# Query-normed attention: the Newton steps of its two unit lengths issued in GpSimd's list instead of VectorE's

## The chip, the cores and the metric

The kernel runs on one core of a Trainium2 chip. The metric is the device time of one execution, in microseconds (us); the median of several executions is quoted. The core has four compute engines that work side by side, each through its own list of instructions in order: TensorE (PE, matrix products and transposes), VectorE (DVE), ScalarE (ACT, activations and copies) and GpSimd (POOL). PEld in the profile is TensorE's weight load, SP the engine that issues most DMAs. An instruction that waits holds up everything behind it in its engine's list.

## What is computed

A decoder of four blocks of three sublayers on a stream X of 32 sequences of 128 tokens, 128 features each, all float32. Each sublayer adds its output to X. The change lies in the third sublayer ("L0f"), an attention whose softmax is normed over the queries, followed by two products, each scaled to rows of unit length, and a GELU:

```python
x = x + L0_ffn(layernorm(x), Wq, Wk, Wv, Wo, Wff)
def _l2_normalize(z):
    n = jnp.linalg.norm(z, axis=-1, keepdims=True)
    return z / jnp.maximum(n, EPS)
def L0_ffn(x, Wq, Wk, Wv, Wo, Wff):          # 16 heads of 8
    q, k, v = split_heads(x @ Wq), split_heads(x @ Wk), split_heads(x @ Wv)
    scores = jnp.einsum('bqd,bkd->bkq', q, k) / jnp.sqrt(D)
    attn = jax.nn.softmax(scores, axis=-1)    # over the queries
    out = jnp.einsum('bkq,bkv->bqv', attn, v)
    z = merge_heads(out) @ Wo
    z = _l2_normalize(z)
    z = z @ Wff
    z = _l2_normalize(z)
    return jax.nn.gelu(z, approximate=False)
```

## The kernel before

The first five sublayers run as one software pipeline, the method `stream`. Its unit of work is one sequence n; four sequences make a group g, so L0f has 32 sequences in 8 groups. The pipeline counts steps t. In step t the scores of sequence t are made, and each of the other functions works on an earlier or a later sequence, by the offsets in the two tuples `after` and `ahead`. A function of a group runs when the last (for `after`) or first (for `ahead`) sequence of the group is at its offset, so each runs every fourth step.

The order on every engine is the order in which the program is written. While `stream` runs, each engine is wrapped in a `Lane` (its call is line 1350, which is why nearly all instructions of the profile carry that line) that ties every instruction to the one written before it for that engine.

```python
after = ((last, 11), (units, 10), (third, 9), (second, 8), (units, 6), (closed, 5), (features, 4))
ahead = ((turned, 5), (queries, 3), (keyed, 2), (valued, 1), (normed, 9))
```

For a sequence of L0f (kind "keys"):

- `scores` makes its scores (PE, tile `sc`), takes the exponential (ACT, tile `PT`, two instructions) and adds the two halves of the queries on GpSimd (tile `half`, two instructions of 128x512).
- `summed`, one step later, finishes that sum on VectorE (tile `rcs`: a reduction and a reciprocal) and has GpSimd multiply the values by it (tile `vs`).
- `values`, another step later, multiplies `PT` by `vs` on PE (tile `av`).

For a group: `closed` (Wo) and `third` (Wff) make a product, which ACT copies to `z` and squares with sums of rows to `ss`. `units`, one step later, calls `unit` (lines 1699 to 1706): VectorE clamps `ss`, calls `rsqrt` (line 1814) for the reciprocal root of four numbers on each partition, and multiplies each of the four 128x128 pieces of `z` by its column of the result. `units` stands in `after` twice, at 10 and at 6: in one step the second unit length of an older group is made and then the first unit length of a younger one. Such a step is called a slot here. The eight groups make nine slots, four steps apart: the first and the last with one call, the seven between with two. Behind the calls of a slot, VectorE's list has half of `queries` (tile `qTm`), then `summed` of the sequence before; GpSimd's list has `half` of the slot's own sequence, then `vs` of the sequence before. In front of the slot GpSimd's list has `half` of the sequence before and `vs` of the one before that.

`rsqrt` takes a first guess by integer arithmetic in `guess` (line 1806, two VectorE instructions, tile `ry`) and refines it by three Newton steps on the engine that it is given, with a scratch tile `rt`. VectorE, which is the default, takes three instructions a step, GpSimd four. The same helper is already given GpSimd elsewhere in the kernel (line 2129 for four numbers a partition, lines 2023 and 2324 for 32).

Of the kernel before, what the change touches and what calls it, by code (L numbers as in the profile page):

```python
# [1366 lines left out]
class Fast(General):  # L1367
# [125 lines left out]
    def stream(self, stages, context=False, fresh=False):  # L1493

        tc, plain = self.tc, self.nc
        nc = self.nc = Ordered(plain, tc)
        M = NB * len(stages)
        with ExitStack() as es:
            wk = es.enter_context(tc.tile_pool(name="st", bufs=2))
# [199 lines left out]
            def unit(s, name):  # L1699

                nc.vector.tensor_scalar(s["ss"], s["ss"], 1e-24, None, ALU.max)
                rn = self.rsqrt(wk, s["ss"], "u")
                z = wk.tile([128, 4, 128], F32, tag=name, name=name)
                for j in range(4):
                    nc.vector.tensor_scalar(z[:, j, :], s["z"][:, j, :], rn[:, j:j + 1], None, ALU.mult)
                return z
# [23 lines left out]
            def units(g):  # L1730
                st, s = T[g // 8], G[g]
                if st["kind"] == "keys":
                    s["unit"] = unit(s, "z1")
# [39 lines left out]
            for t in range(-9, M + 12):  # L1773
# [22 lines left out]
                if fresh:  # L1796
                    for k in range(2):
                        u = t - (M - NB + 8 * k + 13)
# [1438 lines left out]
```

## Time and profile before

| what | value |
|---|---|
| median of 3 executions | 5677.57 us (5674.41 to 5685.71) |
| the profiled execution | 5680.26 us |
| its span in the profile | 5678.4 us |
| PE busy | 5087.1 us (90%) |
| DVE busy | 4253.1 us (75%) |
| POOL busy | 3060.6 us (54%) |
| ACT busy | 2941.2 us (52%) |
| L0f's slots in the trace | from 335 to 533 us |

A timeline row has the start in us, the length in us, the engine, the line, the operation, the tiles (out<-in), the shapes and the number of instructions merged into the row; in brackets, how long the engine sat idle before it and what ended that. A waits row has the waiting engine and tile, what ended the wait, the total in us, how often, and the longest. A windows row has a stretch, its length, and the busy time of PE, PEld, DVE, ACT and POOL in it with the number of instructions, then TensorE's granted clock (1.00 is full), the DMA share and GB/s.

### The profile page before, as it was taken

The page shows a single profiled execution, that of the slowest core. Times are in us where ns is not written, and L with a number is a line of the kernel's source. Part 1 is how long each engine was busy: PE and PEld are TensorE (multiplying, and loading weights), DVE is VectorE, ACT ScalarE, POOL GpSimd, SP SyncE. Part 2 cuts the span into 40 slices and gives each one's busy share as a digit, 9 for nine tenths or more (in the row PEclk, how much of TensorE's full clock was granted, in tenths as well). Part 3 has the DMA queues.
Part 4 walks back from the last instruction along what each step waited for, and adds up shares of the span by engine and source line. Part 5 has one row for each costly group of instructions (what it writes and reads, how often), then busy time and mean ns, then how long its engine had stood idle before and what let it go on. Part 6 is the DMA issues. An engine that isn't in the chain of part 4 may idle for free.

```text
span 5678.4 us, 143610 instructions
## 1 busy us (share of the span) xinstructions
PE 5087.1 (90%) x56814; PEld 3545.0 (62%) x56814; DVE 4253.1 (75%) x11590; ACT 2941.2 (52%) x4126; POOL 3060.6 (54%) x4772
## 2 busy tenths in 40 slices
PE   8978976877868998986899999999999999999998
PEld 4544556755646666663666666666666666666665
DVE  5587642255538999986888888888888888888885
ACT  5767642334425555543455555555555555555553
POOL 0041011021015555546777777777777777777774
PEclk9989977888989999998999999999999999999999
DMA  1000065324002222212334444444444444444442
GB/s 50 2 1 2 24 202 164 99 64 116 5 20 52 52 55 50 50 40 56 63 62 85 83 76 72 80 78 73 70 83 76 70 80 80 71 70 72 73 74 52
DMA packets 1807430, 376.01 MB, mean 66 GB/s; under 512 B 1681458, under 2 KB 1786393, under 8 KB 1805726
## 3 DMA queue, kind: packets, MB, share of 16 engines
q1 hardware_dynamic: 1797376, 330.90, 28.8%
q10 hardware_dynamic: 4766, 19.06, 1.0%
q0 software_dynamic: 4608, 16.78, 0.9%
q8 instruction: 451, 7.39, 0.6%
q14 instruction: 229, 1.88, 0.1%
HBM read 124.02 MB, written 41.16 MB: 29 GB/s over the span
## 4 chain that ended last, share of the span: by engine, by line
PE 36%; DVE 12%; SPq 8%; POOL 5%; DMA 4%; issue 4%; ACT 2%; DVEq 0%; ACTq 0%; POOLq 0%
SPq L2039 7%; PE sc L1350 6%; PE y L1350 6%; PE av L1350 5%; PE qk L1350 5%; PE vp L1350 4%; DMA qkT<-bt 3%; POOL rt L1350 2%; DVE bt L1350 2%; POOL raw L1350 2%; PE gp L1350 2%; PE oTp L1350 2%; PE ap L1350 1%; DVE ss L1350 1%; DVE neg L1350 1%
## 5 line engine op out<-in xcount | busy, mean ns | idle before, releaser
L1350 POOL TENSOR_TENSOR raw<-raw,rt 128x1024 f32<-128x1024 f32 x384 | 899.7, 2364 | 0.0
L1350 POOL TENSOR_TENSOR raw<-raw,ry 128x2048 f32<-128x2048 f32 x224 | 811.7, 3624 | 14.0
L1350 PE MATMUL qk<-wqkv,zs 128*128 128x512 f32 x1536 | 725.0, 594 | 7.0 <-DVE raw L1350 7.0
L1350 ACT ACTIVATE sq<-qk 128x1024 f32<-128x1024 f32 x448 | 458.8, 1024 | 363.4 <-PE qk L1350 152.6
L1350 POOL TENSOR_TENSOR rt<-ry 128x32 f32<-128x32 f32 (+1 forms) x864 | 200.3, 232 | 794.1 <-DVE ry L1350 685.2
L1350 DVE TENSOR_REDUCE ss<-sq 128x16 f32<-128x1024 f32 x448 | 532.6, 1194 | 52.0 <-ACT sq L1350 52.0
L1350 DVE TENSOR_TENSOR rt<-qk,tab 128x1024 f32<-128x1024 f32 x384 | 468.4, 1220 | 59.4 <-ACT sq L1350 38.7
L1350 DVE STREAM_TRANSPOSE bt<-raw 128x1024 f32<-128x1024 f32 x384 | 455.3, 1221 | 71.4 <-POOL raw L1350 44.7
L1350 DVE TENSOR_TENSOR raw<-qk,tab 128x1024 f32<-128x1024 f32 x384 | 466.3, 1214 | 0.0
L1350 ACT ACTIVATE PT<-sc 128x1024 f32<-128x1024 f32 x384 | 373.3, 1029 | 127.9 <-PE sc L1350 126.0
L1350 PEld LDWEIGHTS qk<-wqkv,zs 128*128 128x128 f32 x1536 | 274.2, 191 | 263.4 <-issue 255.2
L1350 ACT ACTIVATE P<-sc 128x1024 f32<-128x1024 f32 x384 | 373.3, 1022 | 119.6 <-PE sc L1350 119.1
L1350 ACT COPY oT<-oTp 128x512 f32<-128x512 f32 x384 | 208.7, 589 | 437.4 <-PE oTp L1350 437.4
L1350 PE MATMUL sc<-qkT 64*128 64x128 f32 x6144 | 406.7, 283 | 7.1 <-DMA qkT<-bt 1.4
L1350 PEld LDWEIGHTS sc<-qkT 64*128 64x128 f32 x6144 | 374.5, 193 | 58.8 <-issue 53.4
L1350 PE MATMUL vp<-wqkv,zs 128*128 128x512 f32 x768 | 403.7, 607 | 1.4 <-DVE raw L1350 1.4
L1350 PE MATMUL av<-va,P 128*64 128x65 f32 x12288 | 401.6, 223 | 0.0
L1350 PE MATMUL y<-wo,oT 128*128 128x128 f32 x3072 | 389.9, 280 | 0.0
L1350 PEld LDWEIGHTS av<-va,P 128*64 128x64 f32 x12288 | 375.0, 137 | 23.2 <-issue 0.2
L1350 PEld LDWEIGHTS y<-wo,oT 128*128 128x128 f32 x3072 | 362.2, 192 | 41.8 <-issue 23.9
L1350 ACT COPY va<-vp 128x1024 f32<-128x1024 f32 (+1 forms) x232 | 218.1, 940 | 211.6 <-PE vp L1350 211.3
L1350 POOL TENSOR_TENSOR X<-X,brep 128x512 f32<-128x512 f32 x24 | 30.5, 1272 | 503.9 <-DVE xn L1350 503.9
(414 smaller groups left out, 10754.6 us busy)
## 6 DMA issues: line engine op xcount, KB each, us to landing
qkT<-bt SPq DMA_DIRECT2D x3072, 64.0 KB
rows<-scr SPq DMA_DIRECT2D x32, 672.0 KB
tup<-whole SPq DMA_DIRECT2D x32, 512.0 KB
gt<-tup SPq DMA_DIRECT2D x64, 256.0 KB
tab<-in_tdo SPq DMA_DIRECT2D x32, 512.0 KB
T<-flt SPq DMA_DIRECT2D x16, 1024.0 KB
wqkv<-in_dqkv ACTq DMA_DIRECT2D x6, 1536.0 KB
scr<-dots SPq DMA_DIRECT2D x128, 66.0 KB
```

Source lines behind the costliest of these rows:

```text
L1350: self.last = call(*a, **k)
L2039: nc.sync.dma_start(out=qkT[r:r + 32, :, j, :], in_=bt[32 * j:32 * j + 32, o])
```

## The change

`unit` hands `rsqrt` GpSimd as the engine of the Newton steps. The clamp of `ss`, the two instructions of the guess and the four scalings of `z` stay on VectorE.

```diff
             def unit(s, name):
 
                 nc.vector.tensor_scalar(s["ss"], s["ss"], 1e-24, None, ALU.max)
-                rn = self.rsqrt(wk, s["ss"], "u")
+                rn = self.rsqrt(wk, s["ss"], "u", nc.gpsimd)
                 z = wk.tile([128, 4, 128], F32, tag=name, name=name)
                 for j in range(4):
                     nc.vector.tensor_scalar(z[:, j, :], s["z"][:, j, :], rn[:, j:j + 1], None, ALU.mult)
```

The helper, unchanged:

```python
def rsqrt(self, wk, v, name, eng=None, y=None):
    nc, n = self.nc, v.shape[-1]
    eng = eng or nc.vector
    y = self.guess(wk, v, name) if y is None else y
    t = wk.tile([128, n], F32, tag="rt" + name, name="rt")
    for _ in range(3):
        eng.tensor_tensor(t, y, y, ALU.mult)
        if eng is nc.gpsimd:
            eng.tensor_tensor(t, t, v, ALU.mult)
            eng.tensor_scalar(t, t, -0.5, 1.5, ALU.mult, ALU.add)
            eng.tensor_tensor(y, t, y, ALU.mult)
        else:
            eng.scalar_tensor_tensor(t, t, -0.5, v, ALU.mult, ALU.mult)
            eng.scalar_tensor_tensor(y, t, 1.5, y, ALU.add, ALU.mult)
    return y
```

## The prediction

> **What bounds the stage now.** The change touches only L0f, so I looked for its nine slots first (VectorE's rows on the tile `ss`: 335.3, 353.5, 380.2, 405.9, 432.4, 459.1, 486.0, 506.4 and 529.3 us) and then read the busy times by stretch, from one slot's second scaling to the next one's, and the waits from 330 to 540 us.
>
> ```profile
> 416.50:443.00 26.50, 20.66 (x196) 12.35 (x196) 22.44 (x70) 16.52 (x34) 11.75 (x12) 0.75 0.00 1
> 443.00:469.80 26.80, 17.45 (x200) 10.38 (x196) 24.29 (x70) 20.35 (x37) 11.89 (x12) 0.93 0.01 2
> ...
> PEld av L1350 <- POOL vs L1350: 58.1, 18, 7.9
> POOL half L1350 <- ACT PT L1350: 41.7, 13, 4.9
> PE av L1350 <- POOL vs L1350: 41.5, 17, 7.1
> POOL vs L1350 <- DVE rcs L1350: 40.1, 13, 7.0
> ```
>
> A group takes some 26.5 us, and VectorE (the third busy time) fills 22 to 24 of them; PE, ACT and GpSimd have room. PE waits for `vs`, GpSimd makes `vs` when VectorE has made `rcs`, and VectorE comes to that `rcs` only behind the slot. So the loop runs through the slot in VectorE's list. The chain that ended last begins only at 1673 us and says nothing here; but from 540 to 700 us PE is busy 151.8 of 160 us, so what is lost in L0f isn't made up behind it.
>
> GpSimd is half idle, which looks like room for the Newton steps. What decides is where they stand in its list. VectorE's rows of the slot at 432 us, then GpSimd's:
>
> ```profile
> 432.52 0.17 DVE L1350 TENSOR_SCALAR ry<-ss 128x4 int32<-128x4 int32 x1
> 432.72 0.17 DVE L1350 TENSOR_SCALAR ry<-ry 128x4 int32<-128x4 int32 x1
> 432.92 0.16 DVE L1350 TENSOR_TENSOR rt<-ry 128x4 f32<-128x4 f32 x1
> ...
> 434.70 3.10 DVE L1350 TENSOR_SCALAR z<-z,ry 128x128 f32<-128x128 f32 x4
> ...
> 437.90 1.23 DVE L1350 TENSOR_SCALAR ry<-ss 128x4 int32<-128x4 int32 x1
> ...
> 442.17 0.87 DVE L1350 TENSOR_SCALAR z<-z,ry 128x128 f32<-128x128 f32 x4
> 442.96 1.41 DVE L1350 TENSOR_SCALAR qTm<-qp,c_small 128x512 f32<-128x512 f32 x2
> ```
>
> ```profile
> 434.86 2.49 POOL L1350 TENSOR_TENSOR half<-PT 128x512 f32<-128x512 f32 x2 [3.58 <-ACT PT L1350]
> 437.30 0.41 POOL L1350 TENSOR_TENSOR vs<-v,rcs 128x128 f32<-128x128 f32 x1
> 437.84 2.50 POOL L1350 TENSOR_TENSOR half<-PT 128x512 f32<-128x512 f32 x2
> ```
>
> The first guess is ready at 432.89. In front of the slot in GpSimd's list stand a `half` and a `vs`; this `half` waits for ACT until 434.86 and the `vs` ends at 437.71. Newton steps written into that list start there, 4.8 us after VectorE is ready for them. The next `half` (437.84) is written behind the slot and will start behind its Newton steps.
>
> The rows also show a collision. Four scalings take 0.87 us alone and 3.10 while `half` runs; a guess takes 0.17 alone and 1.2. VectorE gets about one such instruction through for each `half` instruction of 1.25 us. The reduction (1.2 us) and `qTm` (1.4 us) keep their lengths beside `half`.
>
> **What is removed and added.** Sixteen calls, each 9 VectorE instructions at a pitch of 0.197 us (from 432.92, the first, to 434.70, the scalings behind: 1.78 us): 28 us off VectorE's busy time. Each gets 12 GpSimd instructions. Their form exists later in this trace, four numbers a partition behind the same guess:
>
> ```profile
> 2588.41 0.17 DVE L1350 TENSOR_SCALAR ry<-ry 128x4 int32<-128x4 int32 x1
> 2588.66 0.20 POOL L1350 TENSOR_TENSOR rt<-ry 128x4 f32<-128x4 f32 x1 [8.70 <-DVE ry L1350]
> ...
> 2591.76 0.20 POOL L1350 TENSOR_TENSOR ry<-rt,ry 128x4 f32<-128x4 f32 x1
> ```
>
> So 0.08 us from guess to first instruction and 3.30 from there to the root (2588.66 to 2591.96). The way back to VectorE I put at 0.05: `half` ended at 430.92 and the reduction waiting for it started at 430.95. A root costs 3.43 us where it cost 1.78. It is the same work on the path, slower, and nothing covers it: behind the guess VectorE's list has the scalings, which need the root, and behind them the second call, `qTm` and `rcs`, for which `vs` and PE wait.
>
> **A slot with two calls.** From the end P of the `vs` in front: 0.08 + 3.30 + 0.05 to the first root, 0.87 for its scalings (GpSimd is idle then, as its next instruction waits for the second guess), 0.59 for the clamp and the second guess, 0.08 + 3.30 + 0.05 to the second root: 8.32 us. Then GpSimd starts the held-back `half` in the same moment as VectorE the second scalings, and these take 3.10 as in the row at 434.70: P + 11.42. At 432 us that is 437.71 + 11.42 = 449.13, where the second scalings ended at 443.04: +6.1.
>
> The Trainium skill speaks against this placing as well ("SBUF — State Buffer", section "Who interferes with whom"): of a VectorE instruction in a 2-port mode and a GpSimd instruction, whoever issues first has the shared ports for the whole instruction and the other blocks fully. The row at 434.70 agrees with it (3.10 against 0.87 us); by the rule, an order in which all scalings issue first would save the difference, and the sum would be that of the first rival below.
>
> The other slots by the same sum, with P and the end of the second scalings as they are: 353 us: 358.69 + 11.42 against 364.24, +5.9; 380 us: 384.18 against 390.64, +5.0; 406 us: 411.26 against 416.53, +6.1; 459 us: 463.09 against 469.81, +4.7. (In those of 380 and 459 us VectorE's Newton instructions themselves collided with `half` before, 1.2 us instead of 0.16, which the change takes away; that is in their smaller loss.) The first slot has one call, its guess ready at 337.54 and P at 337.52: 337.54 + 3.43 + 3.10 = 344.07 against 340.22, +3.9. The six: 31.7 us.
>
> Does each loss pass on whole? From the `vs` behind a slot (445.92) to the next P (463.09) are 17.2 us of PE, ACT and GpSimd: `av`, transposes and products, scores, squares on ACT, exponentials, `half`, all in order behind that `vs`. VectorE needs from 445.5 (its `rcs`) to 459.6 for its own way to the next guess and will go on to wait 3.5 us or more there. So P moves with `vs`, and every slot adds its own loss.
>
> **The last three slots** have no `half` behind them, as the next sublayer has none. At 486 us VectorE ends at 486.71 + 9.19 = 495.90 (scalings at 0.87 here) instead of 492.57. PE's transposes wait for the bank that `qTm` frees (494.1, now 497.3), but the product behind them already waited 2.45 us for ACT's copy until 497.64, and now starts at about 498.6: +1. At 506 us VectorE is 3.3 late, `qTm` done at 517.5, and PE wants that bank at 517.70: 0. At 529 us one call, +1.6, of which PE's wait for ACT at 539.4 leaves some 0.5 to 1. Bounds for the three: 0 and 8.3 (3.3 + 3.3 + 1.6); I take 2, by the waits just read.
>
> **The clock.** PE's wait for `vs` grows by the slot's loss. The granted clock is already down in these stretches (0.75 and 0.93 above): behind the 6.8 us wait at 394 us `av` took 1.93 us where 1.08 is its usual length. Behind the 3.1 us wait at 367.8 it took 1.59, so one slot may still get slower. I take 0.5; the bounds are 0 and 1.3 a slot (the spread of `av`, products and scores behind the waits at 367.8 and 420.1), 5 at most.
>
> The Trainium skill ("TensorE: Matmul & The Clock Gate", section "Part 1: The HAM clock gate") has the array fall to half rate after an idle window of about 3.4 us; an estimate by it is the same, since all slots but the first two are past that already.
>
> **The sum.** 31.7 + 2 + 0.5 = 34 us. On the profiled execution that is a span of 5678.4 + 34 = 5712 and a time of 5680.3 + 34 = 5714. That execution stands 2.7 us above the median of the three, so the forecast for the median is 5677.6 + 34 = 5711.6, or 0.6% slower; 5711 in round numbers.
>
> **Rivals.** First: the second scalings don't collide, because VectorE gets its four through before `half` starts, or ACT brings that `half` late. Each of the first six slots is then 2.2 us better: 34 - 13.4 = 21, time 5698. Against it stand three of the double slots before (355.8, 408.3 and 434.7), where scalings that began up to 0.2 us ahead of `half` still took 3.1. In the same direction lies some slack that I don't see between slots.
>
> Second, heavier: the cold PE and the last three slots cost their upper ends, 31.7 + 8.3 + 5 = 45, time 5723.
>
> Third, hidden: VectorE's list isn't what sets the pace and the delays go into existing waits; the 10% that VectorE is idle speaks for it. Then only a few us remain: 5678 to 5686. Against it: PE's 41.5 us of waits for `vs`, the longest right behind the slots.
>
> Fourth, on the other side: P comes ahead of the guess. The place is the `half` in front of the slot. If VectorE's later arrival let ACT and GpSimd run ahead until that `half` and `vs` end before the guess, a double slot would take 9.19 us from the guess, 432.89 + 9.19 = 442.08 against 443.04: a gain of about 1 in each of five, as the collisions go. The point from which it decides is P 4 to 5 us earlier relative to the guess. With 2 lost at the end it gives 5677.6 - 5 + 2 = 5675. Against it: that `half` waits for an exponential which is downstream of the last slot's `vs`. That the Newton steps don't move isn't possible: the wrapped engine that `unit` passes is the one `rsqrt` compares with, so its four-instruction branch is taken.
>
> **Chances.** Forecast 0.60, first rival 0.20, heavier 0.09, hidden 0.07, fourth 0.04. About 0.2%, 11 us, is what a measurement of this kernel can tell from no change. Forecast, first and heavier are all slower by more, 0.88 with a little taken off for the first's lower end; hidden and most of the fourth are within, 0.09; faster by more than 11 us has no mechanism here, 0.03. The range takes in the first rival and most of the unknown ends: 5692 to 5721.
>
> **What would show it.** Right: GpSimd's `rt<-rt,ss` of 128x4 in 48 rows from 337 to some 565 us, the first of each double slot directly behind a `vs`; VectorE idle before `z` for about 8 us (first call) and 3.4 (second), released by GpSimd's `ry`; second scalings of 3.1 us beside `half`; groups of 30 to 33 us instead of 26.5; PE's waits for `vs` up by 25 us or more; rows from 700 us on alike, shifted. Wrong: second scalings of 0.87 (first rival); Newton rows that start right at the guess (fourth); groups still at 26.5 us (hidden).

## The result, and the profile after

| | before | changed |
|---|---|---|
| median | 5677.57 us (5663.06 to 5687.01, 7 runs) | 5704.45 us (5697.33 to 5714.75, 7 runs) |
| span of the profiled execution | 5678.4 us | 5702.7 us |
| DVE busy | 4253.1 us | 4219.8 us |
| POOL busy | 3060.6 us | 3091.2 us |

The change makes the kernel slower: the ratio of the times is 1.005, with a 95% interval of 1.0035 to 1.0065, which is 20 to 37 us. VectorE did get 33 us of work less, and that bought nothing.

Busy times by stretch, changed kernel, each from the end of one slot's second scalings to the next one's (the columns as in the table before: PE, PEld, DVE, ACT, POOL, clock):

```profile
402.40:433.40 31.00, 18.80 (x196) 11.04 (x196) 18.00 (x52) 18.30 (x35) 16.50 (x36) 0.78 0.01 2
433.40:465.60 32.20, 21.31 (x196) 12.35 (x196) 17.27 (x52) 18.30 (x35) 16.36 (x36) 0.71 0.00 1
```

A group takes 31 to 32 us instead of 26.5, and no engine is busy for more than two thirds of it. VectorE, which filled 22 to 24 of 26.5 us, has 17 to 19 of 31 to 32. Who waits, from 330 to 570 us:

```profile
PEld av L1350 <- POOL vs L1350: 81.1, 18, 12.0
DVE z L1350 <- POOL ry L1350: 76.9, 16, 8.4
PE av L1350 <- POOL vs L1350: 65.2, 17, 11.2
```

The second row is new: VectorE stands 76.9 us in front of its 16 sets of four scalings, waiting for GpSimd's root. PE's wait for `vs` went from 41.5 to 65.2 us, by 24 us, most of the loss.

One slot (the one at 432 us before), VectorE's timeline and then GpSimd's:

```profile
449.61 0.17 DVE L1350 TENSOR_SCALAR ry<-ry 128x4 int32<-128x4 int32 x1
457.99 0.88 DVE L1350 TENSOR_SCALAR z<-z,ry 128x128 f32<-128x128 f32 x4 [8.21 <-POOL ry L1350]
...
459.19 0.17 DVE L1350 TENSOR_SCALAR ry<-ry 128x4 int32<-128x4 int32 x1
462.74 2.88 DVE L1350 TENSOR_SCALAR z<-z,ry 128x128 f32<-128x128 f32 x4 [3.38 <-POOL ry L1350]
```

```profile
451.88 2.49 POOL L1350 TENSOR_TENSOR half<-PT 128x512 f32<-128x512 f32 x2 [3.71 <-ACT PT L1350]
454.32 0.41 POOL L1350 TENSOR_TENSOR vs<-v,rcs 128x128 f32<-128x128 f32 x1
454.69 0.20 POOL L1350 TENSOR_TENSOR rt<-ry 128x4 f32<-128x4 f32 x1
...
462.51 0.20 POOL L1350 TENSOR_TENSOR ry<-rt,ry 128x4 f32<-128x4 f32 x1
462.66 2.48 POOL L1350 TENSOR_TENSOR half<-PT 128x512 f32<-128x512 f32 x2
```

The guess is ready at 449.78. GpSimd takes it up at 454.69, behind a `half` that waited for ACT's exponential and behind a `vs`. VectorE waits 8.21 us for the first root and 3.38 for the second. GpSimd's next `half` then starts at 462.66 beside the second scalings, which take 2.88 us where the first took 0.88.

Where the loss arises, by the end of the second scalings of each slot (the only scalings in the first and the last) in the two traces: +1.6 us at the first slot, then 5.4, 4.8, 5.2, 5.7 and 5.0 in the five double slots with half-sums, 3.2, 0.5 and 0.4 in the last three: 31.7. The first gather of the sublayer behind (GpSimd's first indirect DMA into the tile `whole`) starts at 694.6 us before and at 725.0 after: +30.4. The tile's rows, before and changed (durations in ns, then the first and the last start in us):

```profile
L1350 POOL DMA_INDIRECT whole<-in_tup,rows x32: 935/939/1150, 694.6 to 932.2; - x32
L1350 POOL DMA_INDIRECT whole<-in_tup,rows x32: 932/936/1147, 725.0 to 962.8; - x32
```

From there to the end the two traces take 4983.8 and 4977.7 us; the same stretch varies from 4968 to 4984 us in the experiments, in no order, so the difference of 6 us lies within the scatter behind the changed stage. The gather is therefore the sharper gauge, and it is used below.

### The profile page after: what moved, and what is told of

It is laid out like the page before. It is cut to its first block, busy times and chain, and to the rows that moved or that the text cites. A ratio compares the mean times of both kernels' runs of the same rounds, so it can differ in the third digit from the quotient of the medians.

```text
span 5702.7 us, 143664 instructions
## 1 busy us (share of the span) xinstructions
PE 5082.3 (89%) x56814; PEld 3543.1 (62%) x56814; DVE 4219.8 (74%) x11446; ACT 2942.4 (52%) x4126; POOL 3091.2 (54%) x4964
## 5 line engine op out<-in xcount | busy, mean ns | idle before, releaser
L1350 POOL TENSOR_TENSOR rt<-ry 128x4 f32<-128x4 f32 (+1 forms) x912 | 208.3, 228 | 841.6 <-DVE ry L1350 729.9
L1350 PEld LDWEIGHTS y<-wo,oT 128*128 128x128 f32 x3072 | 362.1, 192 | 42.0 <-issue 24.3
```

What stands on the lines that cost most here:

```text
L1350: self.last = call(*a, **k)
```

## The experiments

All are edits of the changed kernel or of the kernel before, and all compute the same. Their diffs are shortened ("..." marks lines left out). First in one table. "Stage" is the time from GpSimd's first `half` to the first gather, against that of before (694.6 - 297.0 = 397.6 us). "A group" is the mean of the five intervals between the clamps of the second to the seventh slot. The ratio comes from runs side by side with the kernel before (its median was 5673.36 us beside e1 to e4, 5677.91 beside e5 and b1 to b3, 5677.28 beside b4 and b5) and isn't exactly the quotient of the medians.

| kernel | first `half` | first gather | stage | a group | median, ratio to before (95%) |
|---|---|---|---|---|---|
| before | 297.0 | 694.6 | 0 | 26.5 | |
| changed | 297.1 | 725.0 | +30.3 | 31.7 | 1.0050 (1.0035 to 1.0065) |
| e1 front half-sum behind | 297.2 | 718.7 | +23.9 | 29.4 | 5691.68, 1.0041 (1.0027 to 1.0054) |
| e2 second call only | 297.1 | 704.1 | +9.4 | 27.8 | 5682.43, 1.0017 (1.0008 to 1.0026) |
| e3 first call only | 299.0 | 718.9 | +22.3 | 30.0 | 5690.71, 1.0035 (1.0022 to 1.0049) |
| e4 own half-sum last | 297.1 | 718.4 | +23.7 | 29.5 | 5692.9, 1.0037 (1.0023 to 1.0051) |
| e5 both held back | 297.2 | 710.6 | +15.8 | 27.7 | 5688.76, 1.0021 (1.0012 to 1.003) |
| b1 before, own half-sum last | 297.0 | 693.8 | -0.8 | 24.9 | 5674.5, 0.9999 (0.999 to 1.0008) |
| b2 before, joint root | 297.3 | 685.0 | -9.9 | 24.3 | 5665.8, 0.9981 (0.9972 to 0.9989) |
| b3 before, joint, own last | 297.1 | 680.4 | -14.3 | 23.1 | 5664.09, 0.9978 (0.9968 to 0.9987) |
| b4 before, joint, late | 297.4 | 705.2 | +10.2 | 25.4 | 5684.44, 1.0008 (0.9999 to 1.0017) |
| b5 joint, late, GpSimd | 300.4 | 715.9 | +17.9 | 27.1 | 5697.61, 1.0032 (1.002 to 1.0043) |

The times of a kernel scatter by some 10 us, so the traces carry the fine differences, one trace for each kernel. The stage and the ratio, taken of 5677.57 us, agree within 4 us in all rows but b4's (+10.2 and +4.5).

**The two calls apart.** e2 leaves the older group's call (the first of a slot) on VectorE, e3 the younger group's:

```diff
-                    s["unit"] = unit(s, "z1")
+                    first = "unit" not in s
+                    s["unit"] = unit(s, "z1", nc.gpsimd if first else None)      # e3: if not first
```

> Newton steps on GpSimd only in the call for the younger group (the second of a double slot, the only one of the first slot); the older group's stay on VectorE. Theory: GpSimd is past its waiting half-sum by the time of the second guess, so a double slot loses only the slower root less the collision it avoids, 1.6 to 1.7 us, the first slot 1.6, the last ones 1.6 in all: gather at 694.6 + 11.5 = 706 us, time 11 us above before. Rival (each call costs the same): half of the whole loss, 15 us: 710 us.

> Newton steps on GpSimd only in the call for the older group (the first of a double slot, the only one of the last slot). Theory: this call carries the wait for the half-sum, and the next half-sum then collides with the first scalings: 2.8 to 4.3 us in each of the five double slots (18 in all), nothing in the first slot, 2 in the last ones: gather at 694.6 + 20 = 715 us, time 20 us above before. Rival (each call costs the same): 15 us, 710 us.

Stages of +9.4 and +22.3 us, against the 11.5 and 20 of the theory and 15 each of the rival; their sum, 31.7, is close to the whole change. Eight calls with the same 12 instructions each cost more than twice as much in the one place as in the other. So the instructions alone don't decide: 12.9 us of the loss is the difference between the two places.

**The half-sum in front taken away (e1).** The `half` of the sequence before the slot is written behind the slot's calls (`halved` has the two additions that stood in `scores`, and `E[n]` is the sequence's `PT`):

```diff
-                    for h in (slice(0, 8), slice(8, 16)):
-                        nc.gpsimd.tensor_tensor(half[:, h], PT[:, h, 0:64], PT[:, h, 64:128], ALU.add)
+                    if n % 4 == 0: held.append(n)
+                    else: halved(n, PT)
...
+                if t % 4 == 1:                          # behind the functions of `after`
+                    while held:
+                        n = held.pop()
+                        halved(n, E[n])
```

> The changed kernel, with one thing moved: the half-sum of the sequence before a slot is written into GpSimd's list behind the slot's Newton steps instead of in front of them. Theory (the place in the list: Newton steps wait 0 to 5 us for that half-sum and its wait for ACT): the first root of a double slot follows its guess by 3.4 us, the slot ends guess + 8.3 + 2.9 us (the second scalings still collide, now with this half-sum), a loss against the kernel before of 1.0 to 1.2 us in each of the five double slots with half-sums, 1.6 to 2 in the first, some 3 in the last three: the first gather of the stage behind (694.6 us before, 725.0 with the change) at about 704 us, and the time about 10 us above the kernel before. Rival (the slow GpSimd instructions, 12 at 0.28 us for 9 at 0.20 on the path, 1.65 us in each of 16 calls): no part of the loss depends on the place, the gather stays at 720 to 725 us.

The stage lost 23.9 us: neither the 10 of the theory nor the 25 and more of the rival. The wait did go: VectorE waits 3.39 us for each first root instead of about 8. But GpSimd's and VectorE's rows behind the second root of a slot show what came in its place:

```profile
427.80 0.20 POOL L1350 TENSOR_TENSOR ry<-rt,ry 128x4 f32<-128x4 f32 x1
427.95 4.92 POOL L1350 TENSOR_TENSOR half<-PT 128x512 f32<-128x512 f32 x4
428.04 4.92 DVE L1350 TENSOR_SCALAR z<-z,ry 128x128 f32<-128x128 f32 x4 [3.38 <-POOL ry L1350]
```

Two half-sums are now held back by the Newton steps, run back to back, and the four second scalings sit among them for 4.92 us. My expectation had counted one of the two. Of a group's 5.2 us, e1 takes back 2.3.

**The other collision taken away (e4).** The slot's own `half` is written behind the `vs` of `summed`, so that it can't start before VectorE is through:

```diff
+                    if n % 4 == 1: held.append(n)
+                    else: halved(n, PT)
...
                     summed(t - 1)
+                while held:
+                    n = held.pop()
+                    halved(n, E[n])
```

> The changed kernel, with the half-sum of the slot's own sequence written into GpSimd's list behind the multiplication by the sums of the sequence before, so that it no longer starts beside the second scalings. Theory: the second scalings take 0.87 us instead of 2.87 and each of the five double slots gets 2.0 us shorter, passed on whole: gather at 725 - 10 = 715 us, time about 17 to 20 us above the kernel before. Rival (the collision isn't on the path that sets the pace, or the later half-sum makes a new wait as long): 722 to 727 us.

The gather came at 718.4, a gain of 6.6 us; the theory had 10, the rival 0. A slot's two scalings now read alike:

```profile
455.38 0.88 DVE L1350 TENSOR_SCALAR z<-z,ry 128x128 f32<-128x128 f32 x4 [6.64 <-POOL ry L1350]
...
460.13 0.87 DVE L1350 TENSOR_SCALAR z<-z,ry 128x128 f32<-128x128 f32 x4 [3.38 <-POOL ry L1350]
```

The group shrinks by 2.2 us, as expected (31.7 to 29.5). What is missing of it at the gather was lost ahead of these five groups: the first slot's clamp starts 2 us later than in the changed kernel (337.36 against 335.39), and the second slot's comes 22.9 us behind it instead of 19.7. The half-sums of the steps in front were moved too; VectorE's reductions at 305.5 and 326.7 us wait 2.38 and 3.08 us for them.

**Both held back (e5).** The edit of e1 with one condition more, and e4's place for the slot's own half-sum:

```diff
-                    if n % 4 == 0: held.append(n)
+                    if n % 4 < 2: held.append(n)
...
                     summed(t - 1)
+                while t % 4 == 1 and held:
+                    n = held.pop()
+                    halved(n, E[n])
```

> The changed kernel with both orders of the earlier runs: the half-sum in front of a slot goes behind its Newton steps, and the slot's own half-sum behind the multiplication by the sums. Theory: what the first experiment still lost was the two half-sums running back to back beside the second scalings (4.92 us there); with one of them gone these take 2.87, a double slot ends 11.7 us after its clamp starts (10.5 to 10.75 in the kernel before, 13.7 in the first experiment), and from its clamp to the first gather the stage takes 359.3 + 10 = 369 us (before 359.3, changed 389.6, first experiment 382.4). Rival (the slow instructions are on the path whatever stands around them): 380 us or more.

From the clamp to the gather it took 710.6 - 338.06 = 372.5 us, beside 369 of the theory and 380 or more of the rival. VectorE's rows of a double slot:

```profile
361.51 0.10 DVE L1350 TENSOR_SCALAR ss<-ss 128x4 f32<-128x4 f32 x1
365.56 0.87 DVE L1350 TENSOR_SCALAR z<-z,ry 128x128 f32<-128x128 f32 x4 [3.39 <-POOL ry L1350]
...
370.30 2.88 DVE L1350 TENSOR_SCALAR z<-z,ry 128x128 f32<-128x128 f32 x4 [3.38 <-POOL ry L1350]
```

The second scalings take 2.88 us and the slot 11.7 (361.51 to 373.18), as worked out. With one half-sum out of the way of the roots and the other out of the way of the scalings, the change loses 15.8 us instead of 30.3. So about half of the loss is the place in GpSimd's list, through the wait and the second collision.

By the clamps the five groups lose only 6.0 us of their 26.1; there the slower root is left, 3.4 us of waiting in front of each scaling where VectorE's own steps took 1.8, with one collision a slot. Another 8.0 us is lost up to the second slot (its clamp at 361.51, 353.49 before). Most of that goes with the order and not with the root: b1 and b3 below, with a half-sum moved and the steps on VectorE, lose 4.7 and 5.0 us there, the changed kernel 1.6. The kernel before wasn't run in e5's order, so the half isn't a split at one order. In e4's order both were run: there the change costs 24.6 us of stage (e4 against b1) and 4.6 a group.

**What helps instead.** The same reading says what would speed up the kernel before: fewer instructions in VectorE's list, fewer collisions. b1 applies e4's order to it. b2 makes one call of a slot's two (`squares` writes both groups' `ss` into one tile of eight columns; one clamp, one guess, nine Newton instructions). b3 does both.

```diff
-                ss = wk.tile([128, 4], F32, tag="ss", name="ss")
+                if at == 0 or "ss" not in T:
+                    T["ss"] = wk.tile([128, 8], F32, tag="ss", name="ss")
+                ss = T["ss"][:, at:at + 4]               # 0 in third, 4 in closed
...
+                rn = self.rsqrt(wk, ss, f"u{hi - lo}")   # once a slot
```

> The kernel before, Newton steps on VectorE, with the slot's own half-sum written behind the multiplication by the sums of the sequence before. Theory (the collisions with the half-sums cost VectorE's list some 4 us a slot, half of them from this half-sum): each of the five double slots is 2.0 us shorter, the reduction that then waits for the later half-sum (1 us) uses up VectorE's present wait for the transposes (1.06 us): from the first clamp to the first gather 359.3 - 10 = 349 us, time 10 us below before. Rival (the later half-sum only moves the wait): 358 to 361 us.

> The kernel before, Newton steps on VectorE, with both calls of a double slot made as one: one clamp, one guess and one set of nine Newton instructions for eight numbers a partition. Theory: the cost is the number of instructions in VectorE's list, not their size, so twelve instructions at 0.2 us less, 2.2 to 2.4 us, in each of seven slots, the last of them absorbed: 359.3 - 14 = 345 us from the first clamp to the first gather, time 14 us below before. Rival (VectorE's list doesn't set the pace): 359 us.

> Both changes of the two runs before together, Newton steps on VectorE. Theory: all eight scalings meet only one half-sum, a double slot is 4.4 us shorter, five times, and 2.7 us more come from the last slots: 359.3 - 25 = 334 us from the first clamp to the first gather, time 25 us (0.4%) below before. Rival: the gains don't add, since behind a shorter VectorE list the chain from the multiplication by the sums through PE and ACT to the next half-sum sets the pace: 345 us.

From the first clamp to the first gather the three took 357.0, 349.4 and 343.4 us. b1 is close to the rival's case: a gain of 1.6 us a group, given back in front of the first slot (its clamp 1.5 us late), between the first and the second (21.4 us against 18.2) and at the end, and its waits from 336 to 520 us show a new one:

```profile
POOL vs L1350 <- DVE rcs L1350: 60.9, 11, 8.8
...
DVE rcs L1350 <- POOL half L1350: 10.1, 8, 3.1
```

VectorE waits 10.1 us for half-sums that now come later, where it had waited 1.4. b2 gains 9.9 us of the expected 14: the twelve instructions of 128x8 have the pitch of 128x4 (0.20 us), but VectorE now waits in four of its slots for the squares on ACT (1.24 to 1.39 us in three, 4.64 in the eighth, 2.43 there before). VectorE's rows of one:

```profile
355.13 0.17 DVE L1350 TENSOR_SCALAR ss<-ss 128x8 f32<-128x8 f32 x1 [1.24 <-ACT sq L1350]
...
361.69 1.66 DVE L1350 TENSOR_SCALAR z<-z,ry 128x128 f32<-128x128 f32 x8
```

The slot is 8.2 us long (355.13 to 363.35), 10.75 before, and 1.24 us of the gain is a wait for ACT in front of it. b3 gains 14 to 16 us, not 25. That is close to its rival's time (345) but not its reason: in the same stretch b1 and b2 gain 2.3 and 9.9 us, and b3's 15.9 is more than both together. The expected sum was too high because its parts were. Both b2 and b3 beat the kernel before, by 0.19% (0.11 to 0.28%) and 0.22% (0.13 to 0.32%), and the changed one with it; which of the two is better isn't settled.

**Other work between the guess and the scalings (b4, b5).** b4 is b2 with the call at the end of the slot's step, behind `summed`. b5 makes the joint call too, with its Newton steps on GpSimd: clamp and guess at the slot's start, Newton steps behind `vs`, scalings and `last` at the end of the next step.

```diff
                     summed(t - 1)
+                if t % 4 == 1: newton(t)                 # b4: units(t), on VectorE
+                if t % 4 == 2:                           # b5
+                    units(t - 1); last(...)
```

> The joint call of b2 (one root for both groups, Newton steps on VectorE), written at the end of the slot's step, behind the sums of the sequence before, instead of at its start. Theory: VectorE then waits some 2.5 us in each slot for the half-sum in front (it comes to that reduction earlier), PE gets its multiplied values some 5 us earlier, and VectorE's list still sets the pace: about what the joint call gains, less that wait: first gather at 685 to 692 us (694.6 before, 685.0 with the joint call alone). Rival: with the values earlier the chain through PE and ACT becomes the bound at 21 to 22 us a group: 670 us.

> One root for both groups, its Newton steps on GpSimd, but with other work between: clamp and guess on VectorE at the start of the slot, the Newton steps in GpSimd's list behind the multiplication by the sums, the scalings (and the GELU and the addition behind them) at the end of the next step. Theory: what made the change slow is that VectorE's list stands still between guess and scalings; with qTm, two reductions and two reciprocals between them VectorE waits 0 to 2.5 us a slot instead of 11.4, and it has nine instructions less: first gather at 680 to 690 us, not above the same late order on VectorE by more than 5 us, and 35 us below the changed kernel (725.0). Rival (GpSimd's slower steps cost their length wherever they stand): at least 3.4 us for each of 9 slots above b4, 715 us or more.

Both missed: gathers at 705.2 and 715.9 us, where 685 to 692 and 680 to 690 were expected. b5's time is its rival's (715 or more), but 3.4 us of it arose ahead of the stage (first `half` at 300.4), and b5 lies 7.7 us of stage above b4, where the rival asked for 30. The waits of b4 from 336 to 520 us, then those of b5:

```profile
DVE qTm L1350 <- PE sc L1350: 22.5, 5, 5.2
...
DVE qTm L1350 <- ACT qTm L1350: 16.9, 3, 8.1
```


```profile
POOL half L1350 <- ACT PT L1350: 70.4, 17, 8.1
...
PEld zp L1350 <- DVE z L1350: 20.5, 21, 3.7
DVE rcs L1350 <- POOL half L1350: 19.4, 12, 2.6
...
DVE z L1350 <- POOL ry L1350: 12.8, 6, 2.2
```

In b4 VectorE stands 39.4 us in front of `qTm`, a wait that the kernel before doesn't have in this window. So the step "VectorE's list still sets the pace" failed there. In b5 VectorE's wait for the root did fall to 12.8 us (63.3 in the changed kernel in this window), the part that the theory had. But the scalings now come late for their readers: PE waits for `z` with its transposes, and GpSimd waits longer for the exponentials (70.4 us, 40.2 in the changed kernel in this window; b4 has 74.4). The late order is bad by itself: b4's stage is 20.1 us longer than b2's. The 7.7 us from b4 to b5 aren't the price of the engine alone, since b5's scalings and `last` also stand a step later. By their times b4 and the kernel before can't be told apart (0.9999 to 1.0017). Why b4's stage is 10 us longer while its groups are 1.1 us shorter was not followed to the end; parts of it lie between the first clamp and the second (24.2 us, 18.2 before) and between the seventh and the eighth (25.2, 20.3 before).

## Why the prediction was right

The direction, the mechanism and, within its range, the size held: 5704.45 against 5711, +27 against +34.

**What bounds the stage.** VectorE's list, with PE waiting for `vs` behind the slot: b2 shows it from the other side, since twelve instructions less in that list took 2.2 us off each group. Collisions account for little of it: they cost the slot at 353 us some 4.4 us before and b2's at 355 us some 4.1.

**The place.** P, the end of the `vs` in front, was the start of the first root as said: 454.69 directly behind it, in all five double slots with half-sums. The experiments separate it: the first calls alone cost 22.3 us, the second ones alone 9.4.

**The root's price.** 0.08 + 3.30 + 0.05 = 3.43 us from guess to scalings was worked out from rows of another sublayer; VectorE's waits of 3.38 to 3.39 us are that.

**The double slot.** P + 11.42 was expected and P + 10.9 came (454.73 to 465.62), with 2.88 instead of 3.10 for the second scalings and a first Newton step that starts as the `vs` drains. The five added 27.8 us in the sum and 26.0 in the trace.

**The terms that were off.** The first slot: 3.9 expected, 1.6 measured. ACT's exponential released its `half` only at 341.87, behind the scalings, which end at 341.84, so the collision didn't happen there; that is the first rival, in one slot of six:

```profile
341.87 2.50 POOL L1350 TENSOR_TENSOR half<-PT 128x512 f32<-128x512 f32 x2 [0.94 <-ACT PT L1350]
```

The last three: 2 expected, 4.1 measured at the scalings (3.2 of it in the first, where I had put 1) and 2.8 at the gather. The clock term of 0.5 wasn't tested apart; the granted clock in the five stretches was 0.71 to 0.95, 0.75 to 0.93 before. The Trainium skill's rule of half rate after an idle window of about 3.4 us ("TensorE: Matmul & The Clock Gate", section "Part 1: The HAM clock gate") is tested by none of these runs by itself. These leave 30.3 us in the stage; the median's 26.9 is 3.4 us less, which is below the scatter behind the stage and inside the interval of 20 to 37. One sign fell just short: PE's wait for `vs` rose by 23.7 us, where 25 or more had been put.

**The rivals.** The collision-free one (5698) is refused by the scalings of 2.87 us; e4 prices it at 2.2 us a group, as put, but at 6.6 us at the gather, where 13.4 had been put. The hidden one is refused by the groups of 31.7 us. The fourth, P ahead of the guess, is refused by the waits of 6.96 to 8.39 us for the first roots of the five double slots, of which the root itself is 3.39. e1 forces it in another way: the half-sum that doesn't run in front of the slot runs beside its scalings, and the stage still loses 23.9 us. The rival's own case, that half-sum done before the guess, was not run, so its 5675 stays untested as a price.

**The rule on the shared ports** in the Trainium skill ("SBUF — State Buffer", section "Who interferes with whom"), by which of a VectorE instruction in a 2-port mode and a GpSimd instruction the one that issues first blocks the other until it is through, agrees for VectorE: 0.87 us for four scalings alone, 2.87 beside one half-sum, 4.92 beside two. GpSimd's half-sums show no loss of their own in these rows: 2.48 us beside the scalings, 2.49 at 451.88 without them.

## What to carry to other kernels

An engine that is half idle on average isn't free at the moment that matters: look at what stands in front of the moved work in its list, and what that waits for. Where the engine that hands over the work has nothing between its last input and the result, its own time isn't freed but spent waiting, and for numbers as small as four a partition the instruction count sets the price, so making one call of two beats moving either. And work held back on one engine comes out in a burst, beside whatever its neighbour does then.

## What was not expected of the hardware

Twelve dependent GpSimd instructions keep a pitch of 0.28 us whether they have four or eight numbers a partition (b5's rows of 128x8 start 0.28 us apart and take 0.20), as VectorE's keep 0.20 for both. And the prediction's "about one" is almost exact: VectorE's scalings beside GpSimd's half-sums pass one per GpSimd instruction; four take as long as two half-sum instructions (2.48) and a little (2.87), or as long as four (4.92 and 4.92).
